# Layer 1's second graph attention turned node-major, with five samples in flight, in a four-layer graph network

## The chip, the cores and the metric

The kernel runs on one core of one Trainium2 chip. The metric is device time in microseconds for one execution over the whole batch of 32 samples; a median over several executions is given, and lower is better. All arithmetic is fp32.

## What is computed

`x` is (32, 512, 256): 32 samples (graphs) of 512 nodes with 256 features. `adj` is one 512 x 512 adjacency for all samples. Four layers follow one another, each adding to `x` what it computes from `relu(layernorm(x))`:

- layer 0: masked attention with four heads of 64 features;
- layer 1: a linear layer to 512 features, an unmasked graph attention, a linear layer to 256, a masked graph attention, and a residual;
- layer 2: a masked graph attention with four heads;
- layer 3: the same with eight heads of 32 features, with a prior, and an output projection.

The change concerns the second attention of layer 1. In the reference:

```python
def _gat(inp, adj_mask, W, a):
    h = jnp.matmul(inp, W)
    f1 = jnp.matmul(h, a[:F_, 0]);  f2 = jnp.matmul(h, a[F_:, 0])
    e = jax.nn.leaky_relu(f1[:, :, None] + f2[:, None, :], ALPHA)
    e = jnp.where(adj_mask[None, :, :] > 0, e, NEG_INF)
    att = jax.nn.softmax(e, axis=2)
    return jax.nn.elu(jnp.einsum('bij,bjf->bif', att, h))
...
residual = out
out = _gat(jax.nn.relu(out), adj, W_hand, a_hand)
out = jax.nn.elu(out) + residual
return jax.nn.relu(out)
```

So each node gets a weighted mean of the other nodes' `h`, then elu twice, the residual (`o3` in the kernel), relu, and the sum goes onto `x`.

## The kernel before

Each sample is processed alone, in tiles of 128 partitions. A (512 x 256) activation is either node-major (four tiles t of 128 nodes with 256 features) or feature-major (two tiles k of 128 features with 512 nodes). Most temporaries are blocks of 128 x 512 fp32 from one pool (`block`, `BLOCKS` of them), and every product of TensorE goes to one of eight PSUM banks of the same size (`bank`).

No engine's instructions are issued in the order of the source. The functions `layer0` to `layer3` only record steps: `q.vector`, `q.scalar`, `q.tensor`, `q.gpsimd` and `q.sync` are recorders of a planner (`Plan`). After all 32 samples are recorded, `Plan.order` makes one list of all steps, greedily: among the steps whose inputs are there and whose buffers can be had, it takes the one with the earliest possible start and, among equals, the earliest due time. The due time is `sample * PERIOD - tail - URGENT[tile:layer]`, where `tail` is the longest chain that follows the step by the planner's own costs (`cost`). Steps of a sample are released at `STARTS`/`PACE` plus `LAYERS`. A sample may start if it is at most `AHEAD` after the oldest unfinished one, and buffers are held back for older samples (`KEEP`, `OWN`). The order is fixed when the kernel is built; at run time each engine takes its list in order and waits by semaphores. In the profile all recorded steps have one line, L283, so groups are told apart by tile names.

The second attention (`second_gat`) works like this before the change:

- `v` is the product of `o3` with `W_hand` and two further columns, the source and destination scores, copied from PSUM by ScalarE, 258 columns for each of four node tiles.
- `largest`, `on_all` and small steps (`nd`, `ew`) give the unnormalised softmax weights. `p[j]` holds, for 128 source nodes j on the partitions, the weights of all 512 target nodes: an Exp on ScalarE, then a max and the mask on VectorE.
- `inverse_sums` adds the four `p[j]` into `total` on VectorE, turns it by four TensorE transposes into `sm`, sums on VectorE into `rs`, takes the reciprocal, and spreads it by four more transposes and a copy to `rc`, one value for each target node along the free dimension.
- `weighted` multiplies feature-major: for each of two feature blocks m it accumulates four matmuls with 128 columns of `v` stationary and `p[j]` (512 columns) moving.
- `elu2` makes `y = av * rc`, then three ScalarE steps `e` (Relu, Exp, Exp) and two VectorE steps into `yT`, the second adding `o3[m]`.
- `layer1` turns `yT` back node-major by eight transposes into `pt` and adds it onto `x` with a max against 1. The double elu is kept one too large throughout, which is why that max is against 1 and not 0.

The first attention of the layer, `first_gat`, uses `inverse_sums`, `weighted` and `elu2` as well, and stays as it is. In layers 2 and 3 (`separable`) a row of scores goes through DRAM and comes back broadcast as `R`, twelve such blocks a sample; in layer 3 some sums are added by DMAs from GpSimd's queue (`p<-p`). Loads of `x`, of `R` and of the reciprocals `rc` are issued on SyncE's queue (SP).

Of the kernel before, what the change touches and what calls it, by code (L numbers as in the profile page):

```python
# [12 lines left out]
F32 = mybir.dt.float32  # L13
BF16 = mybir.dt.bfloat16
I32 = mybir.dt.int32
AF = mybir.ActivationFunctionType
ALU = mybir.AluOpType
# [3 lines left out]
P = 128  # L21
N = 512
NT = N // P
D = 256
KD = D // P
# [16 lines left out]

PERIOD = 179.0
STARTS, PACE = (0.0, 0.0, 38.0, 159.0), 85.0
LAYERS = (0.0, 4.0, 2.0, 98.0)

URGENT = {
    "pt:0": 192, "mm:0": 49, "total:0": 70, "av:0": 68, "mm:1": 25, "total:1": -78, "rs1:1": 42, "av:1": -7,  # L50
    "p2:1": 104, "p3:2": -95, "total:2": -542, "ue:2": -396, "mv:3": -121, "mm:3": -158, "p3:3": -723,
    "av:3": -527, "total:3": -695,
}
BLOCKS, KEEP = 62, 2
KEEP_BANKS = 0

LATE = 30
# [13 lines left out]
class Plan:  # L71
# [6 lines left out]


    ENGINES = dict(tensor="PE", vector="DVE", scalar="ACT", gpsimd="POOL", sync="SP")  # L80
    HOP, AHEAD = 0.05, 3

    OWN = dict(block=8, bank=2)

    SWITCH = dict(full=0.094, columns=0.12, rows=0.2)

# [70 lines left out]
    def order(self):  # L157
# [19 lines left out]
        to_come = [{} for _ in self.samples]  # L177
        pending, place = {}, {}
        for name, s in owners.items():
            tag = self.tile_tag[name]  # L180
# [10 lines left out]
        oldest = 0  # L191

        def slots(step):

            when, taken = 0.0, {}
            for name in step.touches:
                if name in live:
                    continue
                tag = self.tile_tag[name]
                keep = self.tags[tag][1]  # L200
                reserve = 0
                for s in range(oldest, step.sample):
                    if to_come[s].get(tag, 0):
                        reserve += max(0, min(keep, to_come[s][tag] + held.get((s, tag), 0)) - held.get((s, tag), 0))
                n = taken.get(tag, 0)
                own = self.OWN.get(tag, 0)
                if own:
                    passed = bisect_left(pending[step.sample, tag], place[name]) - n
                    reserve += max(0, min(own, passed))
                if len(free[tag]) - n <= reserve:  # L210
                    return None
                when = max(when, sorted(free[tag])[n])
                taken[tag] = n + 1
            return when

        while len(result) < count:
            best = None
            for engine, waiting in open_.items():
                for step in waiting:
                    if step.sample > oldest + self.AHEAD:  # L220
                        continue
                    start = max(at[engine], step.ready)
                    if engine == "PE" and step.mode != mode:
                        start = max(start, at[engine] + self.SWITCH[mode])
# [5 lines left out]
                    start = max(start, when)  # L230
# [3 lines left out]
            _, start, step = best  # L234
# [6 lines left out]
            for name in step.touches:  # L241
                tag, s = self.tile_tag[name], step.sample
# [110 lines left out]
def gnn_stack_kernel(ctx: ExitStack, tc: tile.TileContext, a: dict, out: bass.AP):  # L353
# [13 lines left out]
    x = a["x"]  # L367
# [4 lines left out]
    def T(ap, rearr, **kw):  # L372
        return ap.rearrange(rearr, **kw)
# [17 lines left out]
    ident = const.tile([P, P], F32, name="ident")  # L391
    make_identity(nc, ident)
    mhalf = const.tile([P, NT], F32, name="mhalf")
    mone = const.tile([P, 1], F32, name="mone")
    eps = const.tile([P, 1], F32, name="eps")
    ones = const.tile([P, P], F32, name="ones")
# [21 lines left out]
    first = ctx.enter_context(tc.tile_pool(name="first", bufs=1))  # L418

    def new_x():  # L420
        return first.tile([P, NT, D], F32, name="x", bufs=4)

    prep_stack = ExitStack()
    prep = prep_stack.enter_context(tc.tile_pool(name="prep", bufs=2))
# [158 lines left out]
    def pipelined(stack):  # L583
# [5 lines left out]
        def block(name):  # L589

            return q.tile(big, [P, N], name, BLOCKS, keep=KEEP, tag="block")

        def blocks(name, n):
            return [block(name) for _ in range(n)]

        def bank(name):
            return q.tile(psum, [P, N], name, 8, keep=KEEP_BANKS, tag="bank")

        def small(name, *free):
            return q.tile(big, [P, *free], name, 4)  # L600
# [5 lines left out]
        def col(t):  # L606
            return slice(t * P, (t + 1) * P)
# [34 lines left out]
        def node_major(w, t, inT, c0, cols):  # L642

            ps = bank("mm")
            for k, b in enumerate(inT):
                q.tensor.matmul(
                    ps[:, :cols], b[:, col(t)], w[:, k, c0 : c0 + cols], start=(k == 0), stop=(k == len(inT) - 1)
                )
            return ps
# [12 lines left out]
        def weighted(v, p):  # L662

            av = bank("av")
            for j in range(NT):
                q.tensor.matmul(av, v[j], p[j], start=(j == 0), stop=(j == NT - 1))
            return av
# [92 lines left out]
        def inverse_sums(p):  # L760

            total = block("total")
            q.vector.tensor_tensor(total, p[0], p[1], op=ALU.add)
            q.vector.tensor_tensor(total, total, p[2], op=ALU.add)
            q.vector.tensor_tensor(total, total, p[3], op=ALU.add)
            sm, rs = bank("sm"), small("rs1", NT)
            for t in range(NT):
                q.tensor.transpose(sm[:, col(t)], total[:, col(t)], ident)
            q.vector.tensor_reduce(rs, T(sm, "p (t k) -> p t k", k=P), axis=AX.X, op=ALU.add)
            q.vector.reciprocal(rs, rs)  # L770
            rc = on_all("rc", rs)
            q.behind(sm)
            return rc

        def elu2(dst, av, rc, residual):

            y = block("y")
            q.vector.tensor_tensor(y, av, rc, op=ALU.mult)
            e = block("e")
            q.scalar.activation(e, y, AF.Relu, scale=-1.0)  # L780
            q.scalar.activation(e, e, AF.Exp, scale=-1.0)
            q.scalar.activation(e, e, AF.Exp, bias=mone)
            q.vector.scalar_tensor_tensor(dst, y, 0.0, e, op0=ALU.max, op1=ALU.add)
            q.vector.tensor_tensor(dst, dst, residual, op=ALU.add)
# [27 lines left out]
                elu2(o2[m], weighted([half(va if m < 2 else vb, j)[:, col(m % 2)] for j in range(NT)], p), rc, o1[m])  # L812
            return o2

        def second_gat(o3):
            v = q.tile(big, [P, NT, D + 2], "v2", 2)
            for t in range(NT):
                q.scalar.copy(v[:, t, :], node_major(wh, t, o3, 0, D + 2)[:, : D + 2])
            d = v[:, :, D + 1]
            nd, mn, ew = largest(d), small("mn", 1), small("ew2", 3, NT)  # L820
            q.vector.tensor_reduce(mn, d, axis=AX.X, op=ALU.min)
            q.vector.tensor_tensor(spread[:, q.sample : q.sample + 1], nd[:, 0:1], mn, op=ALU.subtract)
            q.vector.tensor_scalar(ew[:, 2, :], v[:, :, D], nd[:, 0:1], 0.0, op0=ALU.add, op1=ALU.max)
            q.vector.tensor_scalar(ew[:, 1, :], d, ALPHA, nd[:, 2:3], op0=ALU.mult, op1=ALU.add)
            q.scalar.activation(ew[:, 0, :], d, AF.Exp, bias=nd[:, 1:2])
            r, p = on_all("r2", ew[:, 2, :]), blocks("p2", NT)
            for j in range(NT):
                q.scalar.activation(p[j], r, AF.Exp, bias=ew[:, 1, j : j + 1], scale=ALPHA - 1.0)
                q.vector.scalar_tensor_tensor(
                    p[j], p[j], ew[:, 0, j : j + 1], mask1T[:, j, :], op0=ALU.max, op1=ALU.mult  # L830
                )
            rc = inverse_sums(p)
            yT = blocks("yT", KD)
            for m in range(KD):
                elu2(yT[m], weighted([v[:, j, col(m)] for j in range(NT)], p), rc, o3[m])
            return yT

        def layer1(xt):
            hT = norm_t(xt)
            o1 = blocks("o1", KH)  # L840
            for m in range(KH):
                q.scalar.activation(o1[m], feature_major(m1, m, hT), AF.Relu, bias=b1[:, m : m + 1])
            o2 = first_gat(o1)
            o3 = blocks("o3", KD)
            for m in range(KD):
                q.scalar.activation(o3[m], feature_major(m2, m, o2), AF.Relu, bias=b2a[:, m : m + 1])
            yT = second_gat(o3)
            for t in range(0, NT, 2):
                pt = bank("pt")
                for i in range(2):  # L850
                    for k in range(KD):
                        q.tensor.transpose(pt[:, col(2 * i + k)], yT[k][:, col(t + i)], ident)
                q.vector.scalar_tensor_tensor(
                    xt[:, t : t + 2, :], T(pt, "p (t d) -> p t d", d=D), 1.0, xt[:, t : t + 2, :],
                    op0=ALU.max, op1=ALU.add,
                )

        def separable(xt, w, nh, mask, bars):

# [165 lines left out]
        for i in range(B):  # L1025
            q.begin()
            q.sample, q.left = i, B - i
            xt = q.adopt(new_x() if i else x0, "x", 4)
            if i:
                q.sync.dma_start(xt, xv[i])  # L1030
            for q.layer, layer in enumerate((layer0, layer1, layer2, layer3)):
                layer(xt)
            q.sync.dma_start(ov[i], xt)
# [430 lines left out]
```

## Time and profile before

| | before |
|---|---|
| median of 3 executions | 3960.19 us (3959.78, 3960.19, 3964.37) |
| span of the profiled execution | 3962.9 us |
| TensorE (PE) busy | 3890.9 us, 98% |
| its weight loads (PEld) | 2149.1 us, 54% |
| VectorE (DVE) busy | 3344.2 us, 84% |
| ScalarE (ACT) busy | 2805.9 us, 71% |
| GpSimd (POOL) busy | 566.4 us, 14% |
| mean granted TensorE clock | 0.992 |

The span runs from the first to the last instruction of one execution. The listed times don't say which execution was profiled; only the one of 3964.37 us is longer than the span, by 1.5 us, so an execution like the profiled one takes some 1.5 us beside its span. Busy time is the union of the shown durations on an engine. Matmuls are pipelined and their ends are modelled, so the distance from one start to the next is the better price of a matmul. An fp32 matmul shows as two records, a transpose as one; some records can be missing.

### The profile page before, as it was taken

How to read it: one execution, taken by the hardware profiler on the slowest of the kernel's cores; microseconds unless marked ns; L12 is line 12 of the kernel's file. 1: busy time of each engine (PE TensorE's matmuls, PEld its weight loads, DVE VectorE, ACT ScalarE, POOL GpSimd, SP SyncE). 2: the span in 40 equal slices, each digit the busy share in tenths (PEclk: the TensorE clock that was granted, in tenths of full speed). 3: DMA queues.
4: the chain of work that ended last, by engine and by line, in shares of the span. 5: the costliest groups of instructions: out<-in, count | busy, mean ns of one | idle time of the engine just before them, and what ended most of it. 6: DMA issues, size and time to landing. Idle time of an engine off the chain costs nothing.

```text
span 3962.9 us, 52558 instructions
## 1 busy us (share of the span) xinstructions
PE 3890.9 (98%) x17144; PEld 2149.1 (54%) x17144; DVE 3344.2 (84%) x7049; ACT 2805.9 (71%) x5968; POOL 566.4 (14%) x530
## 2 busy tenths in 40 slices
PE   8999999999999999999999999999999999999997
PEld 4655555555555555555555555555555555555552
DVE  6499898888888888988888988888888889888886
ACT  4577677766677766767766777666777667777665
POOL 0001111101111111111101111011111011111010
PEclk8999999999999999999999999999999999999998
DMA  3013333313233223333223333132332233332231
GB/s 101 21 37 81 72 82 84 92 44 92 57 89 92 71 65 76 76 84 84 67 63 78 76 88 88 49 89 59 86 92 73 63 76 76 84 83 69 71 77 50
DMA packets 217616, 292.57 MB, mean 74 GB/s; under 512 B 49915, under 2 KB 103422, under 8 KB 217334
## 3 DMA queue, kind: packets, MB, share of 16 engines
q0 software_dynamic: 68864, 111.18, 16.1%
q1 hardware_dynamic: 148196, 177.69, 14.3%
q8 instruction: 138, 2.26, 0.2%
q14 instruction: 144, 1.18, 0.1%
q10 hardware_dynamic: 274, 0.26, 0.0%
HBM read 158.79 MB, written 19.10 MB: 45 GB/s over the span
## 4 chain that ended last, share of the span: by engine, by line
PE 69%; DVE 17%; DMA 5%; ACT 4%; issue 2%; POOL 2%; SPq 1%; DVEq 0%; ACTq 0%; POOLq 0%
PE mm L283 33%; PE av L283 22%; PE sc L283 5%; PE pt L283 5%; DVE total L283 5%; DVE p L283 5%; DMA R<-rd 4%; PE sm L283 3%; ACT p L283 2%; POOL rs L283 2%; DVE o L283 1%; DVE ue L283 1%; DVE stats L283 1%; DVE x L283 1%; DVE y L283 1%
## 5 line engine op out<-in xcount | busy, mean ns | idle before, releaser
L283 ACT ACTIVATE p<-R,e 128x512 f32<-128x512 f32 x1536 | 993.4, 727 | 53.2 <-DMA R<-rd 52.3
L283 PE MATMUL av<-p,v 128*128 128x512 f32 (+1 forms) x2560 | 930.8, 596 | 4.5 <-DVE p L283 4.4
L283 DVE SCALAR_TENSOR_TENSOR p<-p,e,mask3T 128x512 f32<-128x512 f32 x1024 | 720.5, 749 | 8.1 <-ACT p L283 8.1
L283 POOL TENSOR_TENSOR rs<-ve,mhalf 128x4 f32<-128x4 f32 x128 | 202.5, 1582 | 2755.9 <-DVE ve L283 2634.4
L283 PEld LDWEIGHTS av<-p,v 128*128 128x128 f32 (+1 forms) x2560 | 348.2, 169 | 446.5 <-issue 357.2
L283 DVE TENSOR_TENSOR total<-total,p 128x512 f32<-128x512 f32 x872 | 572.6, 687 | 1.4
L283 PE MATMUL av<-p,vs 128*32 128x512 f32 (+1 forms) x3072 | 504.5, 598 | 5.6 <-DVE p L283 5.4
L283 PE MATMUL mm<-W_fc,o 128*128 128x256 f32 (+1 forms) x2048 | 468.4, 380 | 2.8 <-ACT o L283 2.8
L283 PEld LDWEIGHTS mm<-W_fc,o 128*128 128x128 f32 x2048 | 382.5, 190 | 85.3 <-issue 29.4
L283 POOL DMA_DIRECT2D p<-p x360 | 323.9, 1047 | 564.2 <-PE av L283 191.2
L283 DVE SCALAR_TENSOR_TENSOR p<-p,e,mask1T 128x512 f32<-128x512 f32 x512 | 350.7, 748 | 41.0 <-ACT p L283 40.4
L283 ACT ACTIVATE h<-x,ms,rs 128x256 f32<-128x256 f32 x512 | 280.1, 628 | 122.9 <-DVE ms L283 121.0
L283 DVE TENSOR_TENSOR p<-p,mask0T 128x512 f32<-128x512 f32 x512 | 328.5, 690 | 17.4 <-ACT p L283 17.2
L283 PEld LDWEIGHTS av<-p,vs 128*32 128x32 f32 (+1 forms) x3072 | 138.4, 118 | 342.2 <-issue 238.6
L283 DVE TENSOR_TENSOR total<-p,p 128x512 f32<-128x512 f32 x436 | 288.7, 687 | 0.0
L283 ACT ACTIVATE p<-sc 128x512 f32<-128x512 f32 x512 | 254.3, 679 | 7.8 <-PE sc L283 7.8
L283 PE MATMUL mm<-w,hT 128*128 128x272 f32 (+1 forms) x1024 | 254.4, 393 | 0.9 <-ACT hT L283 0.8
L283 PE MATMUL mm<-hT,mlp_w 128*128 128x512 f32 x512 | 237.6, 596 | 0.0
L283 PE MATMUL mm<-o,mlp_w 128*128 128x512 f32 x512 | 234.7, 596 | 1.3
L283 PE MATMUL sc<-qT,kT 64*128 64x512 f32 x1024 | 230.1, 599 | 0.0
L283 PEld LDWEIGHTS mm<-w,hT 128*128 128x128 f32 x1024 | 190.6, 191 | 61.0 <-issue 15.3
L283 ACT COPY rc<-pt 128x512 f32<-128x512 f32 x64 | 37.4, 585 | 246.8 <-PE pt L283 246.7
(183 smaller groups left out, 5457.5 us busy)
## 6 DMA issues: line engine op xcount, KB each, us to landing
R<-rd SPq DMA_DIRECT2D x384, 256.0 KB
p<-p POOLq DMA_DIRECT2D x360, 256.0 KB, 5.3
x<-in_x_dram SPq DMA_DIRECT2D x32, 512.0 KB
x<-boa POOLq DMA_DIRECT2D x32, 512.0 KB, 5.5
rc<-s SPq DMA_DIRECT2D x128, 128.0 KB
out_dram<-x SPq DMA_DIRECT2D x32, 512.0 KB
rc<-s SPq DMA_DIRECT2D x248, 64.0 KB
s<-sums SPq DMA_DIRECT2D x94, 8.0 KB
```

Source lines behind the costliest of these rows:

```text
L283: getattr(getattr(self.nc, attribute), op)(*args, **kw)
```

## The change

- The weighted sum of the second attention is node-major: for each of four node tiles t, four matmuls with 128 columns of `p[j]` stationary and `v[:, j, :]` moving.
- `v` has 257 columns: 256 values, and a last column of ones, so that column 256 of each product is the sum of the weights. The two score columns go to a small tile `sd`. The values are copied with 1 added, which keeps the double elu one too large as before.
- `total`, `sm`, `rs` and `rc` of this attention go, with their transposes. The reciprocal of the sum is one value for each partition; it and its negative enter as a pointer in the Relu on ScalarE and in the max step on VectorE.
- `e` and `u` are handled for two node tiles at a time. `o3` is turned by eight transposes and added in PSUM layout, in place of the eight transposes of `yT`.
- One more buffer for `x` (5), two blocks fewer (60), `AHEAD` 4, a new reserve `SPARE`, and other values of `PERIOD`, `STARTS`, `PACE`, `LAYERS` and `URGENT`, which move steps of all layers in the order.

```diff
-PERIOD = 179.0
-STARTS, PACE = (0.0, 0.0, 38.0, 159.0), 85.0
-LAYERS = (0.0, 4.0, 2.0, 98.0)
+PERIOD = 107.0
+STARTS, PACE = (0.0, 4.0, 19.0, 123.0), 101.0
+LAYERS = (0.0, 32.0, 34.0, 184.0)
...  (URGENT: 17 entries before, 105 after)
-BLOCKS, KEEP = 62, 2
+BLOCKS, KEEP = 60, 2
-    HOP, AHEAD = 0.05, 3
+    HOP, AHEAD = 0.05, 4
+    SPARE = dict(block=2, bank=1)
...
+                if any(to_come[s].get(tag, 0) for s in range(oldest, step.sample)):
+                    reserve += self.SPARE.get(tag, 0)
...
-        return first.tile([P, NT, D], F32, name="x", bufs=4)
+        return first.tile([P, NT, D], F32, name="x", bufs=5)
...
-        def second_gat(o3):
-            v = q.tile(big, [P, NT, D + 2], "v2", 2)
-            for t in range(NT):
-                q.scalar.copy(v[:, t, :], node_major(wh, t, o3, 0, D + 2)[:, : D + 2])
-            d = v[:, :, D + 1]
+        def second_gat(o3, xt):
+            v, sd = q.tile(big, [P, NT, D + 1], "v2", 2), small("sd2", NT, 2)
+            for t in range(NT):
+                ps = node_major(wh, t, o3, 0, D + 2)
+                q.scalar.activation(v[:, t, :D], ps[:, :D], AF.Identity, bias=ones[:, 0:1])
+                q.scalar.copy(sd[:, t, :], ps[:, D : D + 2])
+            q.vector.memset(v[:, :, D : D + 1], 1.0)
+            d = sd[:, :, 1]
...
-            rc = inverse_sums(p)
-            yT = blocks("yT", KD)
-            for m in range(KD):
-                elu2(yT[m], weighted([v[:, j, col(m)] for j in range(NT)], p), rc, o3[m])
-            return yT
+            for t in range(0, NT, 2):
+                e, u, avs, rs = block("e"), block("u"), [], small("rs2", 2, 2)
+                for i in range(2):
+                    av = bank("av")
+                    avs.append(av)
+                    for j in range(NT):
+                        q.tensor.matmul(
+                            av[:, : D + 1], p[j][:, col(t + i)], v[:, j, :], start=(j == 0), stop=(j == NT - 1)
+                        )
+                    q.vector.reciprocal(rs[:, 0, i : i + 1], av[:, D : D + 1])
+                    q.vector.tensor_scalar(rs[:, 1, i : i + 1], rs[:, 0, i : i + 1], -1.0, None, op0=ALU.mult)
+                    q.scalar.activation(
+                        e[:, i * D : (i + 1) * D], av[:, :D], AF.Relu, bias=ones[:, 0:1], scale=rs[:, 1, i : i + 1]
+                    )
+                q.scalar.activation(e, e, AF.Exp, scale=-1.0)
+                q.scalar.activation(e, e, AF.Exp, bias=mone)
+                for i in range(2):
+                    c = slice(i * D, (i + 1) * D)
+                    q.vector.scalar_tensor_tensor(
+                        u[:, c], avs[i][:, :D], rs[:, 0, i : i + 1], e[:, c], op0=ALU.mult, op1=ALU.max
+                    )
+                pt = bank("pt")
+                for i in range(2):
+                    for k in range(KD):
+                        q.tensor.transpose(pt[:, col(2 * i + k)], o3[k][:, col(t + i)], ident)
+                q.vector.tensor_tensor(u, u, pt, op=ALU.add)
+                q.vector.scalar_tensor_tensor(
+                    xt[:, t : t + 2, :], T(u, "p (t d) -> p t d", d=D), 1.0, xt[:, t : t + 2, :],
+                    op0=ALU.max, op1=ALU.add,
+                )
```

In `layer1` the loop that turned `yT` back and added it onto `x` is gone; the call is now `second_gat(o3, xt)`. In the reading of the scores, `v[:, :, D]` becomes `sd[:, :, 0]`.

## The prediction

> **What bounds the kernel now.** I read the page's busy line first, then busy time by stretches, then the order of time on TensorE for durations, and last the chain of waits in the drain.
>
> ```profile
> PE 3890.9 (98%) x17144; PEld 2149.1 (54%) x17144; DVE 3344.2 (84%) x7049; ACT 2805.9 (71%) x5968; POOL 566.4 (14%) x530
> ```
>
> ```profile
> 500.00:1000.00 500.00, 498.43 (x2204) 277.63 (x2204) 434.00 (x916) 368.88 (x783) 79.83 (x71) 1.00 0.32 76
> ...
> 1500.00:2000.00 500.00, 495.98 (x2185) 278.01 (x2184) 430.15 (x896) 362.09 (x771) 78.89 (x73) 1.00 0.33 78
> ...
> 3800.00:3850.00 50.00, 42.36 (x186) 19.95 (x184) 41.98 (x108) 23.38 (x55) 1.03 (x1) 0.95 0.08 22
> ```
>
> Columns of the stretches after the length: busy us of PE, PE's weight loads, DVE, ACT, POOL, then the granted clock. From 200 to 3800 us PE is busy for 3583.4 of 3600 us at clock 1.00: 16.6 us idle. The fill (0 to 200) has 19.9 us of idle PE, the drain (3800 to 3963) 35.6; together 72.0, which is the span less PE's 3890.9. In the chain of waits the 32-matmul blocks of `sc` recur at 701.81, 941.53 and 1181.83 us: 240.0 us for two samples, 120.0 each. DVE has about 104 us of work in such a period, ACT 88. PE's queue sets the time, so an edit is worth its PE time plus what it does to 72 us of idle.
>
> PE's real prices are start to start, since shown ends overlap:
>
> ```profile
> 1502.43 1.90 PE L283 MATMUL mm<-W_fc,o 128*128 128x258 f32 x8
> 1504.17 1.02 PE L283 MATMUL mm<-hT,mlp_w 128*128 128x512 f32 x2
> ...
> 1540.25 0.60 PE L283 MATMUL sm<-ident,total 128*128 128x128 f32 x4
> 1540.68 2.74 PE L283 MATMUL av<-p,v 128*128 128x512 f32 x6
> 1543.40 0.62 PE L283 MATMUL pt<-ident,rs 128*128 128x128 f32 x4
> 1543.86 7.03 PE L283 MATMUL av<-p,v 128*128 128x512 f32 x16
> 1550.73 0.59 PE L283 MATMUL mm<-woT,oT 128*128 128x256 f32 x2
> ```
>
> A matmul of fp32 is two records, a transpose one. Sixteen 512-column records take 1550.73 - 1543.86 = 6.87 us (0.4294 each); eight 258-column ones 1.74 (0.2175 each); four transposes 0.43 and 0.46.
>
> **PE's part of the change, per sample.** Gone: the four transposes of `total` and the four of `rs`, 0.43 + 0.46 = 0.89 us. The weighted sums turn from 8 matmuls of 512 columns (16 records, 6.87 us) into 16 of 257 (32 records at 0.2175 = 6.96): +0.09. A longer 258-column run, 56 records in 12.37 us (0.2209 each), gives +0.20 as the upper end; nothing excludes a shade under 0.09. The eight transposes before the last add stay, now of `o3`. Net -0.80 us (ends -0.69 and -0.85); 32 samples: -25.6 us (-22 to -27). The weight loads double in number; loads in the 258-column group take 190 ns each against 217 ns between starts, so they stay beneath.
>
> The Trainium skill, TensorEngine Tiling, Instruction Overhead, speaks against the finer cut: about 60 cycles of overhead for each matmul. At the 2.4 GHz of the Trainium skill, TensorE: Matmul & The Clock Gate, the table at its head, I estimate 25 ns, and 16 more records would cost 0.40 us a sample, 13 us in all, with some 16 us left as PE's gain. The trace does not agree: a 258-column record is only 3 ns longer than half a 512-column one.
>
> **DVE and ACT, per sample.** Busy shares come from these groups and their neighbours:
>
> ```profile
> L283 DVE TENSOR_TENSOR total<-total,p 128x512 f32<-128x512 f32 x872 | 572.6, 687 | 1.4
> L283 DVE TENSOR_REDUCE rs<-sm 128x4 f32<-128x512 f32 x64 | 44.3, 693 | 6.1 <-PE sm L283 6.1
> L283 DVE SCALAR_TENSOR_TENSOR yT<-y,e 128x512 f32<-128x512 f32 x64 | 41.8, 692 | 45.8 <-ACT e L283 45.8
> L283 ACT ACTIVATE h<-x,ms,rs 128x256 f32<-128x256 f32 x512 | 280.1, 628 | 122.9 <-DVE ms L283 121.0
> ```
>
> DVE loses three adds of `total` (0.66 each), the reduction (0.69), a reciprocal (0.18), and for two feature blocks `y`, the max and the residual (0.65 each): 6.8 us. It gains four 256-wide max steps (about 0.46: 0.40 for such a step by the `ue` group, 0.06 for the pointer), two 512-wide adds from PSUM (0.66), eight one-column steps (0.11 to 0.17) and a memset (under 0.1): 4.1 to 4.7. Net about -2.4. ACT loses the `rc` copy (0.58), six 512-wide steps (3.87) and four 258-wide copies (1.49); it gains four 256-wide moves with a bias (0.43), four two-column copies (0.15), four Relu (0.55 by the `h` group, which also has two pointers) and two pairs of Exp (2.63): net +1.2. Both engines have 16 and 32 us of slack a sample, so in the steady state I take both at nothing. What hides the +1.2 is PE's queue; on the path it would be 38 us in all, the bound if that cover were gone.
>
> New waits: the max step waits for two Exp while holding two `av` banks. Before, a bank was free after `y` (0.66 us); now after reciprocal, negation, two Relu, two Exp and two max steps, 4 to 5 us. Behind the waiting max steps on DVE stand other samples' p steps, and PE's `av` waits for those. The banks cost 2 of 8 for some 9 us in 120. I take nothing, with 0.5 us a sample (16 us) as the bad end, since PE now waits for DVE's p a mere 9.9 us in the whole run.
>
> **The drain.** The only place where this attention's own chain is bare is the last sample:
>
> ```profile
> 3831.28 3.63 PE av L283 x8
> 3834.91 0.21 PE sm L283
> ...
> 3838.09 0.49 ACT rc L283
> ...
> 3838.60 0.70 DVE y L283
> ...
> 3843.69 0.70 DVE yT L283
> ...
> 3846.25 1.29 DVE x L283 x2
> ```
>
> From the last p (3833.4) to the last `x` (3847.5) are 14.1 us. The new chain needs, after that p, between 1.7 us (only the four last products left) and 7.0 us (all of `av`), then reciprocal and negation 0.3, Relu 1.1 for both halves, Exp 1.3, max 0.9, add and last step 1.4, hops 0.2: 5.2. That ends 2 to 7 us earlier; I take 5.
>
> **Order, fifth sample, two blocks fewer.** No row prices a new order. Below: the 16.6 us in the middle and the 19 us of idle in the drain before 3940. Above: the worst stretch shown after the fill, 4.0 idle in 500 us, over the whole middle would be +12; beyond that lies the first rival. A fifth `x` lets one more sample be held back as filler for the drain, and loads of `x`, which stand in SP's queue ahead of R and `rc` loads, wait less for a buffer. Against it stand 60 blocks instead of 62 and the reserve of `SPARE`. I take -5, a seventh of the drain's idle. The POOL adds and `boa` adds are the same in number, and only their places move.
>
> Sum: -25.6 - 5 - 5 = -35.6 us. The profiled span is 3962.9, 2.7 over the median of 3960.2; of the runs shown only the 3964.4 one can contain it, with 1.5 us around. 3962.9 + 1.5 - 35.6 = 3929 for an execution like the profiled one; taken off the median it is 3925, the number I give.
>
> **Rivals.** *Blocks run short (slower).* Place: the R broadcasts of layers 2 and 3, twelve blocks a sample.
>
> ```profile
> L283 ACT ACTIVATE p<-R,e 128x512 f32<-128x512 f32 x1536 | 993.4, 727 | 53.2 <-DMA R<-rd 52.3
> ```
>
> ACT already idles 52.3 us for them, and one R load of about 8 us stands in the chain in most 240 us periods, covered by other samples' matmuls. With five samples over 60 blocks, R is asked for later and the cover ends first. It decides from 1.1 us of new PE idle a sample, which eats the 35.6; at 1.5 us (48) the time is 3973. For it: the blocks are what the plan runs out of by its reserves. Against: the second attention now holds fewer of them (no `yT`, `total`, `rc`). 0.15.
>
> *PE is not the bound, and its gain vanishes.* If matmul starts were paced by data, the 25.6 would fall away and only the drain's 5 stay: 3955. The Trainium skill, Trainium Kernel Development and Optimization, Performance Expectations, calls matmul busy time a bad metric and wants the share of weight loads, which is 54% here. By that rule PE would have room. Against: 258 and 512 columns cost the same per column, and waits of PE by name sum to some 60 us. 0.15, half of it inside 0.2%.
>
> *The order takes the idle too.* 30 us more out of drain and middle: 3895. For: 35.6 of the 72 lie in a drain where one sample is nearly alone. Against: its last 115 us are a serial path of layers 2 and 3 that the change leaves alone. 0.15.
>
> **The numbers.** The forecast, 3905 to 3945, has 0.55. Faster by over 0.2% (under 3952.3; about what a measurement can tell from no change): 0.55 + 0.15 + 0.06 = 0.76. Within: 0.09. Slower: 0.15. The range 3890 to 3964 takes in the order's good end and most of the second rival, and leaves out the first.
>
> **What would show it.** `sc` blocks recurring every 119.2 us a sample; groups of `sm<-ident,total` and `pt<-ident,rs` halved to 128; 1024 records of `av` at 257 columns, about 0.2175 apart; DVE busy down by 75 us, ACT up by 40; idle PE between 200 and 3800 still under 25 us. Wrong if the 257-column records start over 0.23 us apart, if PE waits for DVE's p or for R by tens of us, or if the drain is longer.

## The result, and the profile after

The changed kernel takes 3902.18 us (median of 4 runs, 3900.39 to 3905.73) against 3961.44 (4 runs, 3959.78 to 3964.37) for the kernel before on the same chip: a ratio of 0.985, 95% interval 0.9836 to 0.9864, 59 us less. The forecast was 3925, 35 us less. The profiled execution took 3905.73 us with a span of 3903.9, against 3962.9 before.

The busy line of the changed kernel's page, and its busy time by stretches (columns as before: PE, weight loads, DVE, ACT, POOL, granted clock, DMA share, GB/s):

```profile
PE 3824.9 (98%) x17400; PEld 2230.5 (57%) x17400; DVE 3292.2 (84%) x7177; ACT 2837.1 (73%) x6128; POOL 519.1 (13%) x530
```

```profile
0.00:200.00 200.00, 180.96 (x713) 108.77 (x714) 112.75 (x288) 100.80 (x204) 15.17 (x21) 0.99 0.23 60
200.00:3740.00 3540.00, 3516.05 (x16037) 2059.91 (x16037) 3053.29 (x6641) 2634.77 (x5715) 488.52 (x494) 1.00 0.32 76
3740.00:3904.00 164.00, 127.89 (x653) 61.83 (x651) 126.14 (x249) 101.54 (x212) 15.44 (x15) 0.90 0.29 74
```

Idle PE did not shrink: 19.0 us in the fill (19.9 before), 24.0 in the middle (16.6), 36.1 in the last 164 us (35.6 in the last 163). The whole gain lies inside PE's *busy* time, which fell by 66.0 us, where the removed and added work accounts for 25.6. So 40 us of what the view before called busy was not work.

The order of time on PE around one `sc` block, changed kernel (start, length, then line, engine, operation, shape, count):

```profile
853.48 5.37 PE L297 MATMUL av<-v,p 128*128 128x257 f32 x24
858.69 1.89 PE L297 MATMUL mm<-L_WoT,oT 128*128 128x256 f32 x8
...
861.71 1.90 PE L297 MATMUL av<-v,p 128*128 128x257 f32 x8
863.45 1.89 PE L297 MATMUL mm<-L_WoT,oT 128*128 128x256 f32 x8
865.17 1.08 PE L297 MATMUL mm<-w,hT 128*128 128x272 f32 x4
866.18 7.14 PE L297 MATMUL sc<-qT,kT 64*128 64x512 f32 x32
```

Twenty-four records of 257 columns take 858.69 - 853.48 = 5.21 us from start to start, 0.2171 each; the eight take 1.74, 0.2175 each. The next `sc` blocks start at 983.78 and 1101.80: 117.6 and 118.0 us a sample, where 119.2 was forecast and about 120 was the pace before.

Groups of the changed kernel (count | busy, mean ns | idle just before, and its releasers):

```profile
L297 PE MATMUL av<-v,p 128*128 128x257 f32 x1024 | 232.6, 380 | 2.7 <-ACT o L297 1.4 <-DVE p L297 1.3
L297 PE MATMUL sm<-ident,total 128*128 128x128 f32 x128 | 19.3, 273 | 0.0
L297 PE MATMUL pt<-ident,rs 128*128 128x128 f32 x128 | 19.2, 273 | 0.0
```

```profile
L297 ACT ACTIVATE p<-R,e 128x512 f32<-128x512 f32 x1536 | 1001.5, 716 | 82.5 <-DVE total L297 75.6
```

The instructions changed as the diff says. The last line is the surprise: ACT's step that reads R idles for a DVE step now, and R is no longer its main releaser. The waits say how far (waiting step, what it waited for: us in total, times, longest), first before, then after:

```profile
ACT p L283 <- DMA R<-rd: 52.3, 42, 5.3
```

```profile
ACT p L297 <- DMA R<-rd: 6.9, 3, 6.1
```

The chain that ended last has become PE's own (it was PE 69%, DVE 17%, with R's loads at 4%):

```profile
PE 85%; ACT 8%; DVE 3%; issue 2%; DMA 2%; POOL 0%; SPq 0%; DVEq 0%; ACTq 0%; POOLq 0%
```

**Where PE's time went, by starts.** Shown ends of pipelined matmuls overlap the next start, so a PE that starts a few hundred ns late still looks busy. I therefore took every PE record's start to the next record's start, over samples 5 to 27 of the trace, and subtracted the record's own length: columns / 1.2 + 2.6 ns (0.4294 us for 512 columns, 0.217 for 257, as in the rows), 109 ns for a transpose, divided by the number of records that run side by side where only part of the rows or columns is used. What is left between two full-array records, if over 60 ns, is a stall; what is left around partial-array stretches (the `sc`, `sm` and `av` steps of layers 0, 2 and 3) holds their switching and their stalls together.

```
us per sample        period   own work   full-array stalls (number)   around partial-array steps
before               120.13    115.62      1.38 (7.0)                   2.91
after                117.97    114.82      0.46 (1.6)                   2.47
difference            -2.16     -0.80     -0.92                        -0.44
```

The remaining 0.2 us are small gaps, equal in both. Own work fell by the 0.80 of the forecast to the digit. The other 1.36 us a sample, 43 us over 32 samples, are mostly short stalls, 0.1 to 0.6 us each, that no view of idle time listed. 32 samples at -2.16 are -69; the fill and the drain together got 10 us longer (span less 32 periods: 118.7 before, 128.9 after).

### The profile page after: what moved, and what is told of

The parts are those of the page before. It is cut to its first block, busy times and chain, and to the rows that moved or that the text cites. A ratio compares the mean times of both kernels' runs of the same rounds, so it can differ in the third digit from the quotient of the medians.

```text
span 3903.9 us, 53766 instructions
## 1 busy us (share of the span) xinstructions
PE 3824.9 (98%) x17400; PEld 2230.5 (57%) x17400; DVE 3292.2 (84%) x7177; ACT 2837.1 (73%) x6128; POOL 519.1 (13%) x530
## 3 DMA queue, kind: packets, MB, share of 16 engines
q14 instruction: 149, 1.22, 0.1%
## 4 chain that ended last, share of the span: by engine, by line
PE 85%; ACT 8%; DVE 3%; issue 2%; DMA 2%; POOL 0%; SPq 0%; DVEq 0%; ACTq 0%; POOLq 0%
PE mm L297 43%; PE av L297 31%; PE pt L297 6%; ACT p L297 6%; PE sm L297 3%; DVE p L297 2%; PE sc L297 1%; DMA p<-p 1%; ACT h L297 1%; DVE total L297 1%; POOL rs L297 0%; DMA rc<-s 0%; DVE x L297 0%; DMA s<-few 0%; DVE rc L297 0%
## 5 line engine op out<-in xcount | busy, mean ns | idle before, releaser
L297 PE MATMUL av<-p,v 128*64 128x512 f32 (+1 forms) x2048 | 697.7, 597 | 6.6 <-ACT v L297 5.4
L297 DVE TENSOR_TENSOR total<-total,p 128x512 f32<-128x512 f32 x808 | 511.3, 686 | 0.1
L297 POOL TENSOR_TENSOR rs<-ve,mhalf 128x4 f32<-128x4 f32 x128 | 155.5, 1220 | 2367.8 <-DVE few L297 858.5
L297 POOL DMA_DIRECT2D p<-p x360 | 342.9, 1314 | 934.3 <-PE av L297 790.4
L297 PE MATMUL mm<-W_fc,o 128*128 128x256 f32 (+1 forms) x2048 | 459.5, 380 | 0.4 <-ACT o L297 0.4
L297 PEld LDWEIGHTS av<-p,v 128*64 128x64 f32 (+1 forms) x2048 | 257.6, 163 | 334.5 <-issue 278.1
L297 DVE TENSOR_TENSOR p<-p,mask0T 128x512 f32<-128x512 f32 x512 | 317.8, 686 | 13.9 <-ACT p L297 13.9
L297 DVE TENSOR_TENSOR total<-p,p 128x512 f32<-128x512 f32 x404 | 267.4, 690 | 39.0 <-PE av L297 22.6
L297 PE MATMUL av<-v,p 128*128 128x257 f32 x1024 | 232.6, 380 | 2.7 <-ACT o L297 1.4
L297 ACT ACTIVATE e<-av,ones,rs 128x256 f32<-128x256 f32 x128 | 65.6, 562 | 220.8 <-PE av L297 108.6
```

The costliest lines, as they stand in the source:

```text
L297: getattr(getattr(self.nc, attribute), op)(*args, **kw)
```

## The experiments

Two theories were to be told apart. *Theory PE*: the attention's removed PE work (and what each microsecond of PE queue drags along) is the gain, and the rest is diffuse. *Theory R*: the new order brings the R broadcasts in time, and that is the larger part; what R's lateness cost before was hidden in PE's short stalls. A third reading, that the fifth sample or the new order as such wins, runs beside both.

### Halves of the change: orders searched anew

The old attention with the diff's other parts; its order was searched anew:

```diff
 # second_gat as before
-BLOCKS, KEEP = 62, 2
+BLOCKS, KEEP = 60, 2
-    HOP, AHEAD = 0.05, 3
+    HOP, AHEAD = 0.05, 4
+    SPARE = dict(block=2, bank=1)
-        return first.tile([P, NT, D], F32, name="x", bufs=4)
+        return first.tile([P, NT, D], F32, name="x", bufs=5)
# PERIOD, STARTS, PACE, LAYERS and URGENT: found by a new search on the plan's length
```

> The feature-major attention of before, with five x, 60 blocks, the reserve, and an order searched for it (plan 3812.5 us; before 3818.9, after 3802.0). Of the 59 us won, 26 are PE work of the attention. Theory A (the other 33 are the order's): 3961 - 33, 3920 to 3940 us. Rival B (the attention's form takes the stalls away as well, the order nothing): 3950 to 3965 us.

4063.79 us, ratio 1.026 (1.0243 to 1.0277): slower by 102, outside everything expected. Waits of this kernel:

```profile
ACT p L298 <- DMA R<-rd: 173.8, 74, 7.6
PE mm L298 <- DVE y L298: 77.0, 47, 3.5
```

So an order that the plan holds for good can leave R more than three times as late as before, and the banks that `y` frees with it. The plan's own length for this order was 3812.5 us, for the kernel before 3818.9 and for the changed one 3802.0: it does not see what separates them on the chip by 160 us. One place of this kernel, in order of time, and the stretch around it:

```profile
2074.29 0.68 DVE L298 TENSOR_TENSOR y<-av,rc 128x512 f32<-128x512 f32 x1
...
2075.03 2.07 PE L298 MATMUL mm<-wvT,hT 128*128 128x256 f32 x4 [2.75 <-DVE y L298]
```

```profile
2070.00:2075.00 5.00, 1.44 (x4) 0.30 (x2) 4.83 (x9) 5.00 (x10) 0.00 (x0) 0.91 0.00 0
2075.00:2079.00 4.00, 3.97 (x7) 2.45 (x8) 3.81 (x7) 4.00 (x8) 0.00 (x0) 0.50 0.00 0
2079.00:2083.00 4.00, 4.00 (x13) 2.71 (x12) 4.00 (x7) 3.39 (x6) 0.00 (x0) 0.76 0.00 0
```

PE waits 2.75 us for `y`, and is charged for it twice: the granted clock of the 4 us behind the wait is 0.50. (The trace has it drop at 2074.12; in the 3.41 us ahead of that PE was busy for 0.73 us.) Over the whole run it is 0.982, against 0.995 in the changed kernel.

The other half, the new attention with four samples of x, 62 blocks, `AHEAD` 3 and no `SPARE`, its order also searched anew:

```diff
 # second_gat as after
-BLOCKS, KEEP = 60, 2
+BLOCKS, KEEP = 62, 2
-    HOP, AHEAD = 0.05, 4
+    HOP, AHEAD = 0.05, 3
-    SPARE = dict(block=2, bank=1)
+    SPARE = dict(block=0, bank=0)
-        return first.tile([P, NT, D], F32, name="x", bufs=5)
+        return first.tile([P, NT, D], F32, name="x", bufs=4)
```

> The node-major attention with four x, 62 blocks, no reserve, and an order searched for it (plan 3796.2 us). Theory A in the form that five samples give the slack: the 26 us of the attention alone, 3925 to 3945 us. A in the form that any order searched anew does it: 3890 to 3910. Rival B (the attention's form alone): 3895 to 3910 us.

3930.69 us, ratio 0.992 (0.9904 to 0.9937): 31 less than before, 28 more than the changed kernel, with R awaited for 63.8 us in 45 places, somewhat more than in the kernel before. That is half the gain, and about what the attention's PE work should bring. The match is in part luck: in the profiled execution (3942.5 us, the slowest of the four) PE's own work is that of the changed kernel, 114.82 us a sample by starts, but the full-array stalls are 2.01 us (1.38 before) and the time around partial-array steps is 1.88 (2.91 before). Another order moves stalls about as well. Most of the 2.01 stand where PE waits for ACT's `kT`:

```profile
PE mm L297 <- ACT kT L297: 28.1, 13, 3.8
```

### What a microsecond of PE is worth

With the order held, each transpose in layer 1 of one kind is issued twice, eight more a sample (the same place in the queue, the same result): `o3` in the changed kernel, `yT` in the kernel before.

```diff
                     getattr(getattr(self.nc, attribute), op)(*args, **kw)
+                    if op == "transpose" and self.kinds.get(args[1].tensor.name) == "o3" and step.layer == 1:
+                        getattr(getattr(self.nc, attribute), op)(*args, **kw)
```

> The changed kernel in its own order, each transpose of o3 issued twice: eight more transposes a sample, 256 in all, 0.109 us each. If PE's queue sets the time, 0.87 us a sample: 3902 + 28 = 3930 us (3924 to 3934). If PE has room (its starts paced by data): 3902 to 3910.

> The kernel before in its own order, each transpose of yT issued twice: the price of the eight transposes that the change removed. If PE's queue sets the time: 3961 + 28 = 3989 us (3983 to 3993). If PE has room, as its 6.9 short stalls a sample might leave it: 3961 to 3970.

3933.48 us (0.9928, 0.9912 to 0.9945), 31.3 more than the changed kernel; and 3993.71 (1.0078, 1.0062 to 1.0095), some 31 more than the kernel before and a shade over the window that I gave. PE's queue sets the time in both, at about 1.1 us for each us of own work by the medians. The executions of one kernel spread over some 8 us here, and by starts the changed kernel's period rises by 0.85 us for 0.88 of own work, so 1.0 is not excluded. The 25.6 us that the attention takes out are then worth 26 to 29 us (25.6 x 31.3 / 28 = 28.6). The rival that PE's gain would vanish is out.

### What R's lateness is worth

With the order held, each R load brings 128 of the tile's 512 columns, and ACT reads those four times; the values differ, the instructions and their places don't.

```diff
+                    if op == "dma_start" and args and self.kinds.get(args[0].tensor.name) == "R":
+                        args = [v[:, :P] for v in args]
+                    if op == "activation" and self.kinds.get(args[1].tensor.name) == "R":
+                        args = [args[0].rearrange("p (a b) -> p a b", b=P), args[1][:, None, :P].to_broadcast([P, NT, P]), *args[2:]]
                     getattr(getattr(self.nc, attribute), op)(*args, **kw)
```

> The kernel before, its order held; of each R only 128 of 512 columns are loaded and read four times, so its values are other ones: a quarter of R's bytes, which land some 4 us sooner for four of them; the work of every engine is the same. Theory R (what the new order won beyond PE's work is that R is there in time; ScalarE waits 52 us for it in before, 7 in after): these waits go and 20 to 40 us with them, 3920 to 3945. Rival S (the short PE stalls of before come from evictions that the old order places just in time, whatever R does): 3953 to 3965.

> The changed kernel, its order held, with the same quarter of R loaded and read (other values). Both theories: little is left to win, since ScalarE waits 7 us for R in all: 3892 to 3904 us. A gain as large as that of the kernel before would say that fewer bytes help in another way than by R's arrival.

The kernel before falls to 3924.66 us (0.9907, 0.989 to 0.9923), 38 less, though nothing on PE has changed; the changed kernel only to 3901.5 (0.9846, 0.983 to 0.9863). The control shows that smaller loads as such win nothing where R is already in time. Waits of the kernel before with cut loads:

```profile
ACT p L287 <- DMA R<-rd: 9.0, 12, 4.8
```

43 us of waits by name went, 38 us of time came back, and by starts the period fell from 120.13 to 118.81: stalls 1.38 to 0.98, around partial-array steps 2.91 to 2.01. Those steps are the `sm` and `av` of layers 2 and 3, which read what ACT makes of R. The 16.6 us of idle PE that the middle of that kernel shows could not have held 38. The chain that ended last says the same. Before, R loads stand in it for 146.4 us between 500 and 3700 us, thirteen of them 7.5 to 9.9 us long, such as

```profile
1019.99 9.01 DMA R<-rd
```

With cut loads there are thirteen of 1.8 to 2.9 us, 32.5 us in all, and in the changed kernel there is none.

Fewer bytes also helped the sums that DMAs add from GpSimd's queue, so that is a rival to R's arrival. GpSimd's waits for them, before and with cut loads:

```profile
POOL p L283 <- DMA p<-p: 96.5, 94, 3.7
POOL p L287 <- DMA p<-p: 14.5, 19, 1.3
```

But the PE steps that read those sums, `sm<-p,ones`, kept their time by starts to 0.01 us a sample. The 0.90 came back in the runs of `sm<-total,ones` (0.49) and of `av<-p,vs` (0.41), and no step of PE waits for a `p<-p` by name in either kernel.

The same cut on the two searched halves:

> The kernel of the new attention with four samples of x (3930.7), its order held, each R load cut to 128 of its 512 columns (read four times, so the values differ). Theory R: the 28.5 us by which that kernel is behind the changed one are its 63.8 us of waits for R, so they fall below 15 us and the time comes to 3898 to 3910. Rival, four samples of x keep PE short of other work whatever R does: 3922 to 3932. Between the two, both have a share and the time is 3910 to 3922.

> The kernel of the old attention in an order searched anew with five samples (4063.8), its order held, each R load cut to 128 of 512 columns (other values). Theory R: its 173.8 us of waits for R and what the clock loses behind them are most of the 101 us by which it is behind the kernel before, so the time comes to 3955 to 3985 at a clock of 0.995 or more. Rival, the order itself starves PE (77 us of waits for the banks that y frees): 4030 to 4064, with y still awaited for over 60 us.

The four-sample kernel falls from 3930.7 to 3895.8 us (0.9833, 0.9817 to 0.9849), 35 less, a little below the window I gave and 6 below the changed kernel with or without the cut, which is within the intervals of the ratios (0.9817 to 0.9849 here, 0.983 to 0.9863 there). Its R waits:

```profile
ACT p L301 <- DMA R<-rd: 13.2, 7, 5.2
```

PE's waits for `kT` are gone, and with them 1.43 us of full-array stalls a sample. That settles the third reading: with R in time, four samples and their order are no worse than five, so the fifth sample by itself wins nothing that these runs show. The four times also cross: the attention is worth 31 us with R late (3962 to 3931) and 29 with R in time (3925 to 3896), R is worth 38 with the old attention and 35 with the new. They add up, as far as kernels with different orders can tell.

The old attention in its searched order falls from 4063.8 to 4000.3 us (1.0093, 1.0077 to 1.011), 63 of the 102 us and a clock of 0.990: less than theory R wanted (3955 to 3985). Its waits:

```profile
ACT p L302 <- DMA R<-rd: 126.3, 39, 7.0
PE mm L302 <- DVE y L302: 46.7, 25, 2.5
```

Even a quarter of the bytes lands late by 126 us in all, so in that order R is asked for late, not only slow to land, and the order starves PE by `y` besides. That it is the blocks which delay the asking was not tried.

### More lateness, and an order that allows for it

Each R load of the changed kernel issued twice, order held:

```diff
+                    if op == "dma_start" and args and self.kinds.get(args[0].tensor.name) == "R":
+                        getattr(getattr(self.nc, attribute), op)(*args, **kw)
                     getattr(getattr(self.nc, attribute), op)(*args, **kw)
```

> The changed kernel, its order held, each R load issued twice: four R land some 5 us later. Theory R: the slack that five samples give is used up, ScalarE's waits for R rise to 50 us and more, and the time by 20 to 70 us, 3922 to 3970. Rival S: R's arrival has little weight, 3900 to 3912.

4774.4 us (1.2049), far outside everything expected. This was a poor instrument: SP's queue waited before the second load into a tile until the first had landed, once for each of the 384 loads, and everything behind it on that queue waited too.

```profile
SPq L299 <- DMA R<-rd: 1151.4, 384, 4.4
```

It prices a blocked SP queue, not a few us of lateness, and says nothing between the theories.

Then the new attention with an order searched under a dearer R, so that the plan itself asks for it earlier:

```diff
 # in cost()
+    if out.tensor.name.startswith("R"):
+        return 0.4, 9.0
# PERIOD, STARTS, PACE, LAYERS and URGENT: found by a new search
```

> The changed kernel with an order searched anew in which R is priced at 9.0 us from issue to landing, not 4.8 (plan 3799.8 us; after 3802.0). Theory R: an order that allows for a late R loses less to what the plan does not see; after lost 100 us beyond its plan: 3870 to 3898. Rival S: orders of equal plan differ by chance, 3900 to 3935 as the other searched orders did.

3954.82 us (0.9979, 0.9969 to 0.9989; ten executions from 3943.98 to 3964.31), a clear miss. R came in time (6.5 us of waits), yet by starts the period of the profiled execution (3963.56 us) is 120.16 us, with 2.57 us of full-array stalls a sample for other things, 1.22 of them ahead of `pt<-ident,mx` and 0.40 ahead of `pt<-ident,ew`:

```profile
PE pt L297 <- DVE mx L297: 29.4, 14, 3.6
PE pt L297 <- DVE nd L297: 7.0, 13, 0.6
```

R in time is not enough; another order can bring stalls of its own that cost as much.

### Is ScalarE covered?

The forecast took ACT's and DVE's changes at nothing. Two runs on the changed kernel, order held. In the first, the four Relu that read `av` in the second attention are issued twice:

```diff
                     getattr(getattr(self.nc, attribute), op)(*args, **kw)
+                    if op == "activation" and step.layer == 1 and self.kinds.get(args[1].tensor.name) == "av":
+                        getattr(getattr(self.nc, attribute), op)(*args, **kw)
```

> The changed kernel, order held, each of the four Relu steps of the second attention that read a bank av issued twice (same values): 2.2 us more of ScalarE a sample, 70 us in all, and each pair of av banks held about 1 us longer. Theory, PE's queue sets the time and the prediction's nothing for ScalarE and the banks holds: 3899 to 3910. Rival, the new steps lie on the path (cover gone): up to 70 us more, 3940 to 3972. In between, 3910 to 3940, the cover is partial.

3970.82 us (1.0021, 1.0011 to 1.003): 69 more, nearly the whole 70. ACT is busy for 73% of the span and yet has no slack at that place. The order of time between the second half's Relu and the `p<-sc` steps, changed kernel:

```profile
864.74 0.56 ACT L297 ACTIVATE e<-av,ones,rs 128x256 f32<-128x256 f32 x1 [3.52 <-DVE rs L297]
...
866.00 0.72 ACT L297 ACTIVATE e<-e,mone 128x512 f32<-128x512 f32 x1
866.18 7.14 PE L297 MATMUL sc<-qT,kT 64*128 64x512 f32 x32
...
867.34 7.95 ACT L297 ACTIVATE p<-sc 128x512 f32<-128x512 f32 x16
...
875.82 0.44 PE L297 MATMUL pt<-ident,h 128*128 128x128 f32 x2 [0.42 <-ACT h L297]
```

ACT takes up `sc` 1.16 us after PE starts it and needs 7.95 us for what PE makes in 7.14; the `h` steps behind it on ACT are then what PE waits for, 0.42 us at `pt` (25.5 us by name in the run, of which 11.3 lie between 200 and 3740 us). The same place with the doubled Relu:

```profile
878.11 2.77 PE L297 MATMUL sc<-qT,kT 64*128 64x512 f32 x8
...
881.20 7.93 ACT L297 ACTIVATE p<-sc 128x512 f32<-128x512 f32 x16
881.24 5.54 PE L297 MATMUL sc<-qT,kT 64*128 64x512 f32 x24 [0.36 <-ACT vs L297]
```

ACT comes 3.09 us after PE's start. PE stands still after eight records until ACT has made its copy `vs`, which stands behind the Relu and Exp on ACT's queue. The 1.9 us of lateness are the same in every sample from 5 to 26 and pass straight into the period (117.97 to 120.01). Of the four extra Relu only the last, 0.60 us, lies directly in that stretch. As I read the order of time, the other three came round by DVE: they delay the first half's Exp, DVE's max steps wait for it (1.74 us at this place), and the reciprocal and its negation for the last Relu stand behind them:

```profile
DVE u L297 <- ACT e L297: 77.0, 63, 5.8
```

That wait is 11.1 us in the changed kernel. In the second run the Relu are taken off ACT: DVE computes min(z, 1) in their place, the negation of the reciprocal goes, and the minus one moves into the bias of the first Exp.

```diff
...  (q.positive: filled in second_gat with the reciprocals and the e tiles)
+                    if op == "tensor_scalar" and self.kinds.get(args[0].tensor.name) == "rs2":
+                        continue
+                    if op == "activation" and id(kw.get("scale")) in self.positive:
+                        self.nc.vector.tensor_scalar(args[0], args[1], self.positive[id(kw["scale"])][1], 1.0, op0=ALU.mult, op1=ALU.min)
+                        continue
+                    if op == "activation" and id(args[0]) in self.positive and kw.get("scale") == -1.0:
+                        kw = dict(bias=self.positive[id(args[0])][1])
                     getattr(getattr(self.nc, attribute), op)(*args, **kw)
```

> The changed kernel, order held, the four Relu steps of the second attention (relu(1 - z) on ScalarE, 0.56 us each, with a negation of the reciprocal on VectorE) replaced by min(z, 1) on VectorE in the same place, the negation dropped, and the minus one put into the bias of the first Exp. The same result. ScalarE loses 2.2 us a sample, VectorE gains four steps of 256 columns from PSUM (0.35 to 0.4) less four of 0.15: about +1.0. Theory, in the order of the changed kernel ScalarE is bare between the last Relu and the p<-sc steps, and its lateness there is what PE waits for at pt<-ident,h (25.5 us by name): PE's waits for h fall below 10 us and the time comes to 3870 to 3888, below both kernels. Rival, VectorE is full in the same stretch (4.00 of 4 us) and takes the place of ScalarE: 3895 to 3940, with DVE u or x as what PE waits for. Second rival, all of it was covered in the changed kernel and only the doubled steps bared it: 3899 to 3906, PE's waits for h unchanged.

3900.9 us (0.9848, 0.9834 to 0.9862), the same as the changed kernel, PE's waits for `h` unchanged (27.2 us). The order of time at the same place:

```profile
860.00 0.16 DVE L305 RECIPROCAL rs<-av 128x1 f32<-128x1 f32 x1
...
861.00 0.47 DVE L301 TENSOR_SCALAR e<-av,rs 128x256 f32<-128x256 f32 x1
...
861.50 1.48 ACT L305 ACTIVATE e<-e,mone 128x512 f32<-128x512 f32 x2 [4.49 <-DVE e L301]
862.38 7.14 PE L305 MATMUL sc<-qT,kT 64*128 64x512 f32 x32
...
863.54 7.95 ACT L305 ACTIVATE p<-sc 128x512 f32<-128x512 f32 x16
```

ACT lost 56 us of busy time and DVE gained 34, and neither shows in the time. But the chain at the sensitive place kept its length: the new DVE step stands behind `x` and statistics steps, so the Exp begin 0.88 us before PE's `sc` (861.50 to 862.38) where they began 0.84 before it, and `p<-sc` again starts 1.16 us after it. So the run shows that ACT's work elsewhere is covered, not that a shorter chain here would win nothing; that was not tried. No run with the reference's values beats the changed kernel by more than this 1 us.

## Why the prediction came out as it did

**The sign, and the rivals.** Faster, as forecast, and no rival came true as priced. The time lies 3 us under the forecast's own band (3905 to 3945) and nearest to the third rival's 3895, but not by its mechanism: that one took the idle out of drain and middle, and neither shrank. The slower rival had the right place and the wrong sign: it put the risk at the R broadcasts, asked for later over 60 blocks. They came earlier. The search of the old attention (173.8 us of waits for R, 4064 us) shows that the risk was real for another order.

**PE's own work: right.** -0.80 us a sample forecast, -0.80 by starts; 257-column records 0.217 apart as forecast; the two transpose groups halved. By the extra transposes its 25.6 us were worth 26 to 29. The doubt that the Trainium skill, TensorEngine Tiling (Array Packing), Instruction Overhead, raised (about 60 cycles for each matmul) would have left own work at -0.49 a sample (0.89 less the estimated 0.40); the trace's -0.80 decides.

**Order and fifth sample: mis-sized, and the step that failed.** The term was -5, with ends of -36 and +12. The runs put R's part at 38 us on the kernel before and 35 on the four-sample kernel, and the rest of the new order at +6 (3895.8 to 3901.5, both with cut loads), which is hardly clear of noise. Going from the kernel before by way of the four-sample kernel, the sum is about -30 for the attention with its own order, -35 for R and +6 for the rest: -59. The steps of such a way must add up; what supports them is that R's two values agree (38 and 35) and that the attention's 29 to 31 is close to the 26 to 29 of its PE work. What led me wrong was the bound: 16.6 us of visible idle in the middle was taken as the most an order could win there. PE's stalls of 0.1 to 0.6 us lie under the shown ends of pipelined matmuls and count as busy. The 52.3 us of ACT's waits for R, which I had shown and called covered by other samples' matmuls, were the better measure: 38 us of time came back with them. I had even read these loads in the chain that ended last, which was the sign that they were not covered. That the range's lower end of 3890 held is luck: the term's end of -36 was made of idle in middle and drain, and the gain came from elsewhere.

**The drain: failed.** It was to be 5 us shorter because the second attention's chain is bare in the last sample. In the new order it isn't. DVE's order of time there, changed kernel:

```profile
3759.86 2.74 DVE L297 SCALAR_TENSOR_TENSOR p<-p,ew,mask1T 128x512 f32<-128x512 f32 x4
...
3772.43 1.41 DVE L297 SCALAR_TENSOR_TENSOR p<-p,e,mask3T 128x512 f32<-128x512 f32 x2
3773.76 1.68 DVE L297 SCALAR_TENSOR_TENSOR u<-av,rs,e 128x256 f32<-128x256 f32 x4
...
3777.14 1.29 DVE L297 SCALAR_TENSOR_TENSOR x<-u,x 128x512 f32<-128x512 f32 x2
```

From the last `p` of this attention (3762.6) to its last `x` (3778.4) are 15.8 us where it was 14.1: `p` steps of another sample's layer 3 stand between. From there to the end it is 125.5 us, against 115.4 before, the "serial path that the change leaves alone". So the place was wrong; whether the 5 us would be right for a bare chain is not shown.

**DVE, ACT and the banks at nothing: borne out in the sum, the reason too general.** DVE's busy time fell by 52 us (75 forecast) and ACT's rose by 31 (40 forecast). The attention as a whole is worth 29 to 31 us in two pairs of kernels with different orders, and PE's work alone accounts for 26 to 29, so little is left for them; moving 56 us off ACT and 34 onto DVE changed the time by 1. But the cover that I named for ACT, 32 us of slack a sample, is not what counts: ahead of the `sc` steps there is none, and 2.2 us a sample more in this attention cost 2.0. The wait that I named for the banks (DVE's max steps waiting for the Exp, others queued behind) is real, 11.1 us in this order, and 77 as soon as ACT is later.

**What stays open.** Why the plan's search with five samples brought R in time and four did not is not shown: the search is judged by a length that does not see it, and in the runs with a fresh search the order differs everywhere. Nor is the 10 us of longer fill and drain traced to one cause. The cut loads took 1.32 us a sample off the kernel before and the change took 1.36 beside its own work, nearly the same sum, but not in the same places (around partial-array steps 0.90 and 0.44): some of the stalls that left with the new order may be other waits than R's.

## What to carry to other kernels

Where PE is "98% busy", take start to start against each record's own length before saying how much idle an order or a load can win; a wait of another engine for a load that stands in the chain that ended last (here ACT's 52 us for R) was the better bound. The size of a wait alone says little: in the kernel before ACT waits longest, 246.7 us, for the `pt` that becomes `rc`, and 121.0 us for `ms`. Price a change's PE work and its order separately, and test a late load by shrinking it with the order held; that took one run and its control, and found two thirds of the gain. Cover belongs to a place in the order, not to an engine's share of busy time: try it with a doubled instruction before calling it slack.

## What the runs showed of the hardware beyond that

- A few us of starved PE are charged twice. In the old attention's searched order PE was busy for 0.73 us of the 3.41 before the drop to 0.50 that is shown above. That kernel ran at 0.98 through its steady state, where before and after, whose stalls are shorter, have 1.00. The Trainium skill, TensorE: Matmul & The Clock Gate, Part 1: The HAM clock gate, says that the clock falls to half after at least one idle window of about 3.4 us; the half agrees, and here the window was not wholly idle and still sufficed.
- The doubled R loads held SP's queue for 384 waits of 3.0 us each (1151.4 / 384) until the first load into the tile had landed. Whether two loads into one tile could overlap without that wait was not tried.
- The sixteen `p<-sc` steps of 512 columns take ACT 7.95 us, 0.50 each back to back, where a single one shows 0.6 to 0.7: ACT's shown lengths overlap as PE's do.
